# Attention block: one of two joins of the softmax sums on GpSimd, the steps behind it a burst later

## Chip, core and metric

The kernel runs on one core of a Trainium2 chip. The time is the device time of one execution in microseconds, as a median over runs. The engines are named as in the profile: PE (TensorE matmuls), PEld (its weight loads), DVE (VectorE), ACT (ScalarE), POOL (GpSimd) and SP (SyncE, which here only issues DMAs). Each engine works through its own queue in order; between engines, an instruction waits on semaphores of others.

## The reference

The input x has 4 images of 512 channels and 48 x 48 = 2304 positions. It is a group norm, a 1x1 convolution to q, k and v, attention with 8 heads of 64 channels over the 2304 positions, another 1x1 convolution and a residual:

```python
hn = _group_norm(x, gn_scale, gn_bias)                 # 32 groups
qkv = einsum('oc,bchw->bohw', qkv_w, hn) + qkv_b       # then to float16
w = einsum('bhct,bhcs->bhts', q * scale, k * scale)
w = softmax(w, axis=-1)
a = einsum('bhts,bhcs->bhct', w, v)                    # then to float32
return x + einsum('oc,bchw->bohw', proj_w, a) + proj_b
```

The softmax divides by the sum of exp(score) over the 2304 keys s, for each query position and head. How these sums are formed and applied is what the change is about. No maximum is subtracted in the fast path: the sums are tested against two limits, and if a test fails a general path (not run here) computes all again.

## The kernel before

Two heads are worked together (a pair), so there are 16 groups g: 4 images times 4 pairs. The queries of a group are cut into blocks j: four of 512 and a last, short one of 256. The keys of a block are gone through in bursts. A burst has three steps; each makes scores of 128 keys for both heads and 512 queries (for the short block 256 keys and 256 queries). A full block has 6 bursts, a short one 3, all together 432. The loop at the end of `fast_path` goes over the bursts n in this order and issues for each engine:

- `scores(n)`: 6 matmuls into three banks (`ps`), and three exponentials on ACT into a tile `p` of 128 x 3 x 1024 f16. There are three such tiles.
- `add(n-1)`: on DVE, the burst before is added to the block's accumulator `acc` (128 x 3072 f16, one buffer). The first burst of a block issues nothing; the second adds two `p` tiles at once (`acc<-p,p`). With the last burst the accumulator's three thirds are joined by two more additions (line 991).
- `values(n-2)`: 6 matmuls of v with `p` into the bank `av`, of which there is one; at the block's end DVE copies it to `avx` (line 968).
- `fill(n)`: other work of PE, from a list in a fixed order with costs and due times: chains for q and k of coming groups (line 711), for v (line 762) and for the output projection of the image before (line 839). All use one bank; DVE empties it after each chain (lines 721, 770, 866). A chain of q, k or v is in two pieces, so it is emptied every second burst; a projection chain is one piece. `fill` also issues small tasks for DVE ahead of that: statistics of the next image (line 610) and its normalization (line 662), in the stretches of the run where an image changes.

The joined sums still have to be added over the 128 partitions, inverted and brought to every partition. If E is the last burst of a block, this is done as follows. `add` of E with its joins comes in iteration E+1. In E+2 `turn` transposes the joined 128 x 1024 in blocks of 32 x 32 on DVE (line 1036), then come values of E and the copy to `avx`, then `fill`, and at the iteration's end `fold`: a sum along rows on DVE (line 1044, tile `part`) and four DMAs that bring its quarters to 32 partitions (`qs`). In E+3 `fill` is issued ahead of `values`, otherwise behind. In E+4 `invert_turned` has DVE's small steps (sum of the quarters, reciprocal, a small transposition, lines 1064, 1073, 1075), two DMAs to a row in DRAM, and POOL's tests of the limits (lines 1086, 1087). In E+5 `spread` broadcasts the row to 128 partitions by two DMAs (`ib<-row`), and in E+6 `divide` multiplies `avx` by it on POOL (line 1130) into the attention output `att`. 77 blocks go this way; the last three blocks of the run have their sums added on PE. The function `ready` tells from which burst after E a block's conversion to 32 bits (ACT, line 833) and its projection may start.

Since queues keep their order, a wait of the transposition on DVE holds back what is issued behind it: the emptying of the filling bank, the row sums and the first add of the next block. That first add in turn frees the `p` tile that ACT needs four bursts after E.

Of the kernel before, what the change touches and what calls it, by code (L numbers as in the profile page):

```python
# [17 lines left out]
ALU = mybir.AluOpType  # L18
# [11 lines left out]
NG = B * NPAIR  # L30
NT = T // P
SCALE = float(np.float16(1.0 / math.sqrt(math.sqrt(D))))
BURST = 3
BEHIND = 2
# [10 lines left out]
NQ = len(QBLOCKS)  # L45
# [422 lines left out]
def fast_path(  # L468
# [12 lines left out]
    nc = tc.nc  # L481

    RES = NC
    SQ = 32
# [424 lines left out]


    open_sums, joined = set(), set()
    av, acc, pts, avx, sums, rowd, ibs = {}, {}, {}, {}, {}, {}, {}

    stream = []
# [7 lines left out]
    def scores(u):  # L922
        g, j, k, _ = u
        o, n = QBLOCKS[j]
        per = QB // n
        qt, kt = qk[g]
        pt = ppool.tile([P, BURST, 2, QB], F16, tag="p", name=f"p_{g}_{j}_{k}")
        for r in range(BURST):
            ps = ps_s.tile([P, 2, QB], F32, tag="ps", name=f"ps_{g}_{j}_{k}_{r}")
            for a in range(per):  # L930
                i = (k * BURST + r) * per + a
                for h in range(2):
                    rows = slice(h * D, (h + 1) * D)
                    nc.tensor.matmul(  # L934
                        ps[:, h, a * n : (a + 1) * n],
                        kt[rows, bass.ts(i, P)],
                        qt[rows, o : o + n],
                        start=True,
                        stop=True,
                    )  # L940
            nc.scalar.activation(pt[:, r], ps, AF.Exp)  # L941
        pts[u] = pt

    def values(u):
        g, j, k, last = u
        b, pr = divmod(g, NPAIR)
        o, n = QBLOCKS[j]
        per = QB // n
        pt = pts.pop(u)
        if k == 0:  # L950
            if j == 0:
                atts[g] = apool.tile([P, T], F16, tag="att", name=f"att_{g}")
            av[0] = ps_av.tile([P, QB], F32, tag="av", name=f"av_{g}_{j}")
        for r in range(BURST):
            for a in range(per):
                i = (k * BURST + r) * per + a
                for h in range(2):
                    lo = h * D
                    nc.tensor.matmul(  # L959
                        av[0][lo : lo + D, :n],  # L960
                        vv[b, pr // 2][:, i, pr % 2 * P + lo : pr % 2 * P + lo + D],
                        pt[:, r, h, a * n : (a + 1) * n],
                        start=(i == 0),
                        stop=(i == NT - 1),
                    )
        if last and u is not stream[-1]:
            avx[g, j] = work.tile([P, QB], F32, tag="avx", name=f"avx_{g}_{j}")
            nc.vector.tensor_copy(avx[g, j][:, :n], av[0][:, :n])

    def add(u):  # L970

        g, j, k, last = u
        pt = pts[u]
        if k == 0:
            acc[g, j] = [pt]
            return
        if j >= NQ - 2 and g == NG - 1 and (last or j == NQ - 1):
            acc[g, j].append(pt)
            return
        before = acc[g, j][0]  # L980
        if k == 1:
            acc[g, j] = [
                work.tile(
                    [P, BURST, 2, QB], F16, tag="acc", bufs=1, name=f"acc_{g}_{j}"
                )
            ]
        t = acc[g, j][0]
        nc.vector.tensor_tensor(t, before, pt, ALU.add)  # L988
        if last:
            for r in range(1, BURST):  # L990
                nc.vector.tensor_tensor(t[:, 0], t[:, 0], t[:, r], ALU.add)  # L991
            joined.add((g, j))

    def add_up(g, j, bank=None, more=False):
# [38 lines left out]

    def turn(g, j):

        nc.vector.transpose(  # L1036
            t_turned(g, j).rearrange("p h n -> p (h n)"),
            acc[g, j][0][:, 0].rearrange("p h n -> p (h n)"),
        )

    def fold(g, j):

        part = small.tile([P, SQ], F32, tag="part", name=f"part_{g}_{j}")
        nc.vector.tensor_reduce(  # L1044
            part,
            t_turned(g, j).rearrange("p h (c k) -> p (h c) k", k=SQ),
            AX.X,
            ALU.add,
        )
        del acc[g, j]  # L1050
        quarters = small.tile([SQ, P // SQ, SQ], F32, tag="quarters", name=f"qs_{g}_{j}")
        for p in range(P // SQ):
            nc.sync.dma_start(quarters[:, p, :], part[bass.ts(p, SQ), :])  # L1053
        sums[g, j] = quarters

    def t_turned(g, j):
        return acc[g, j][0][:, 1]

    def invert_turned(g, j):
        n = QBLOCKS[j][1]  # L1060
# [57 lines left out]
    def spread(g, j):  # L1118
        n = QBLOCKS[j][1]
        row = rowd.pop((g, j))  # L1120
        ib = work.tile([P, QB], F32, tag="rows", name=f"ib_{g}_{j}")
        for h in range(2):
            nc.sync.dma_start(
                ib[h * D : (h + 1) * D, :n], row[h : h + 1, :n].to_broadcast((D, n))
            )
        ibs[g, j] = ib

    def divide(g, j):
        o, n = QBLOCKS[j]
        nc.gpsimd.tensor_tensor(  # L1130
            atts[g][:, o : o + n],
            avx.pop((g, j))[:, :n],
            ibs.pop((g, j))[:, :n],
            ALU.mult,
        )
# [37 lines left out]
    def do_tasks(room):  # L1173
        while tasks and tasks[0][0] <= now[0] and room > 0:
            _, us, run = tasks.popleft()
            run()
            room -= us
# [18 lines left out]
    def ready(b, j):  # L1196

        if b < B - 1:
            return BEHIND + 6
        return BEHIND + (4 if j == NQ - 3 else 5)  # L1200

    def put_convert(b, j):
        end = ends[((b + 1) * NPAIR - 1) * NQ + j]
        put(projs[b, j][0], end + ready(b, j))
# [15 lines left out]
    for b in range(B):  # L1220
        g = b * NPAIR
# [113 lines left out]
    def issue():  # L1335
        us, run = beside.pop(0)[:2]
        run()
        credit[0] -= us

    def fill(n):  # L1340

        idle = beside and beside[0][4] and not beside[0][4]()
        if ended(n - 1):
            room = 1.1 if idle else 0.0
        elif ended(n - BEHIND - 1):
            room = 1.1 if idle else 0.5
        else:  # L1350
            room = 2.4 if idle else 1.1
        do_tasks(room)
        rate, work = 0.0, 0.0
        for us, _, _, _, _, _, need in beside:
            work += us
            left = min(need * per_pair, len(stream) - 4) - n
            rate = max(rate, work / max(left, 1))
        credit[0] = min(credit[0] + rate, 4.0)
        closed = False
        while beside:  # L1360
            us, _, first, last, when, after, _ = beside[0]
            if after > n or (first and closed) or (when and not when()):
                break
            if us > 0.1 and credit[0] < us / 2:
                break
            issue()
            closed = closed or last
# [17 lines left out]
    def block_at(n):  # L1385

        return stream[n][:2] if ended(n) and n not in soon else None

    for n in range(end):
        now[0] = n  # L1390
        while loads and loads[0][0] <= n:
            loads.popleft()[1]()
        summed = block_at(n - BEHIND - 1)
        wanted(stream[n][0])
        scores(stream[n])
        if block_at(n - BEHIND):
            turn(*block_at(n - BEHIND))
        if n > 0:
            add(stream[n - 1])
        if summed:  # L1400

            fill(n)
        if n >= BEHIND:
            values(stream[n - BEHIND])
        if block_at(n - BEHIND - 2):
            invert_turned(*block_at(n - BEHIND - 2))
        if block_at(n - BEHIND - 3):
            spread(*block_at(n - BEHIND - 3))
        if block_at(n - BEHIND - 4):

            divide(*block_at(n - BEHIND - 4))
        if not summed:
            fill(n)
        if block_at(n - BEHIND):
            fold(*block_at(n - BEHIND))
        if n - BEHIND in soon:
            g, j = stream[n - BEHIND][:2]
            sx = rows(g, j, add_up(g, j))
            if n - BEHIND == soon[1]:
                divide_here(g, j, sx, avx[g, j], nc.gpsimd)  # L1420
        if n - BEHIND - 1 == soon[0]:
            check_sums(g, j)
            invert(g, j)
        if n - BEHIND - 2 == soon[0]:
            spread(g, j)
            divide(g, j)
    g, b, j = NG - 1, B - 1, NQ - 1
    n = QBLOCKS[j][1]
# [99 lines left out]
```

## Time and profile before

| | us |
|---|---|
| median of 3 runs | 1629.15 (1628.12 to 1629.5) |
| profiled execution | 1627.3 |
| its span | 1625.6 |
| PE busy | 1574.3 (97%) |
| DVE busy | 1319.5 (81%) |
| ACT busy | 1283.2 (79%) |
| POOL busy | 236.2 (15%) |
| both joins of a block, line 991, 156 instructions | 110.8, each 0.71 |
| transpositions, line 1036, 77 | 94.9, each 1.232 |
| row sums, line 1044, 77 | 92.8, each 1.205 |
| divisions on POOL, line 1130, 78 | 121.5, each 1.558 |

The busy time is that of the profiled execution, as a share of its span, which runs from the first to the last instruction. PE's clock was granted at 0.997 of full speed over the run. Busy times of different engines lie beside each other and don't add up to the span. In the groups of instructions a number after the bar is the idle time of that engine just ahead of them and what ended it; in the timeline each row has a start, a duration, engine, line, operation, tiles, and in brackets the idle time before with what ended it.

### The profile page before, as it was taken

How to read it: one execution, taken by the hardware profiler on the slowest of the kernel's cores; microseconds unless marked ns; L12 is line 12 of the kernel's file. 1: busy time of each engine (PE TensorE's matmuls, PEld its weight loads, DVE VectorE, ACT ScalarE, POOL GpSimd, SP SyncE). 2: the span in 40 equal slices, each digit the busy share in tenths (PEclk: the TensorE clock that was granted, in tenths of full speed). 3: DMA queues.
4: the chain of work that ended last, by engine and by line, in shares of the span. 5: the costliest groups of instructions: out<-in, count | busy, mean ns of one | idle time of the engine just before them, and what ended most of it. 6: DMA issues, size and time to landing. Idle time of an engine off the chain costs nothing.

```text
span 1625.6 us, 28473 instructions
## 1 busy us (share of the span) xinstructions
PE 1574.3 (97%) x11316; PEld 685.0 (42%) x11316; DVE 1319.5 (81%) x1533; ACT 1283.2 (79%) x1398; POOL 236.2 (15%) x434
## 2 busy tenths in 40 slices
PE   6999999999999999999999999999999999999996
PEld 2533434443333533545333353355533334434544
DVE  6278789978788889998778787999878887888885
ACT  3077787788888888887888888888878888888894
POOL 1000101221111111111111111101111121111112
PEclk9999999999999999999999999999999999999998
DMA  7002020000000023420000001343000000005413
GB/s 215 6 14 66 12 63 26 18 16 12 14 19 15 13 66 118 141 67 28 12 15 19 15 12 41 116 139 97 25 15 18 15 19 15 16 24 186 125 61 131
DMA packets 71011, 83.10 MB, mean 51 GB/s; under 512 B 26964, under 2 KB 37076, under 8 KB 70868
## 3 DMA queue, kind: packets, MB, share of 16 engines
q1 hardware_dynamic: 68836, 79.34, 16.0%
q8 instruction: 90, 1.47, 0.4%
q10 hardware_dynamic: 1904, 1.84, 0.4%
q14 instruction: 53, 0.43, 0.1%
q0 software_dynamic: 128, 0.01, 0.0%
HBM read 60.70 MB, written 19.17 MB: 49 GB/s over the span
## 4 chain that ended last, share of the span: by engine, by line
PE 72%; DVE 15%; ACT 4%; DMA 4%; issue 3%; SPq 2%; POOL 0%; DVEq 0%; ACTq 0%; POOLq 0%
PE pqk L711 26%; PE av L959 14%; PE pv L762 14%; PE ps L934 14%; DVE acc L988 4%; PE pr L839 3%; ACT p L941 3%; DVE part L1044 2%; PE ps L711 1%; SPq L1053 1%; DMA qs<-part 1%; DVE r L866 1%; DVE acc L991 1%; DMA r<-x_dram 1%; DVE k L721 1%
## 5 line engine op out<-in xcount | busy, mean ns | idle before, releaser
L941 ACT ACTIVATE p<-ps 128x1024 f16<-128x1024 f32 x1296 | 1231.9, 1027 | 306.7 <-PE ps L934 287.8
L711 PE MATMUL pqk<-x,wqkv 128*64 128x512 f32 (+1 forms) x2464 | 520.2, 552 | 8.8 <-DVE k L721 4.2
L988 DVE TENSOR_TENSOR acc<-acc,p 128x3072 f16<-128x3072 f16 x270 | 485.6, 1798 | 41.4 <-ACT p L941 37.9
L934 PE MATMUL ps<-q,k 64*128 64x512 f16 (+1 forms) x2880 | 359.5, 358 | 5.8 <-ACT p L941 5.1
L959 PE MATMUL av<-p,v 128*64 128x512 f16 (+1 forms) x2880 | 361.0, 364 | 0.4 <-DVE slx L1027 0.3
L762 PE MATMUL pv<-wqkv,x 128*64 128x256 f32 x2304 | 269.0, 380 | 4.6 <-DVE v L770 2.7
L711 PEld LDWEIGHTS pqk<-x,wqkv 128*64 128x64 f32 x2464 | 167.9, 137 | 238.9 <-issue 166.3
L934 PEld LDWEIGHTS <-k 64*128 64x128 f16 x2880 | 107.5, 94 | 297.4 <-issue 249.0
L959 PEld LDWEIGHTS <-v 128*64 128x64 f16 x2880 | 131.9, 109 | 210.6 <-issue 166.4
L762 PEld LDWEIGHTS pv<-wqkv,x 128*64 128x64 f32 x2304 | 159.8, 137 | 99.8 <-DVE v L770 8.5
L1086 POOL TENSOR_SCALAR tin<-tsum 32x32 f32<-32x32 f32 (+1 forms) x154 | 45.0, 292 | 953.1 <-DVE tsum L1064 947.9
L1130 POOL TENSOR_TENSOR att<-avx,ib 128x512 f16<-128x512 f32 (+1 forms) x78 | 121.5, 1558 | 353.4 <-DMA ib<-row 350.7
L988 DVE TENSOR_TENSOR acc<-p,p 128x3072 f16<-128x3072 f16 x79 | 139.8, 1769 | 8.0
L839 PE MATMUL pr<-a,whi 128*128 128x512 f32 (+1 forms) x312 | 121.9, 398 | 9.9 <-DVE r L866 5.0
L991 DVE TENSOR_TENSOR acc<-acc 128x1024 f16<-128x1024 f16 x156 | 110.8, 710 | 5.3
L839 PE MATMUL pr<-a,wlo 128*128 128x512 f32 (+1 forms) x312 | 114.4, 374 | 0.0
L770 DVE TENSOR_TENSOR v<-pv,bv 128x512 f16<-128x512 f32 x72 | 49.5, 688 | 70.0 <-PE pv L762 69.8
L721 DVE TENSOR_SCALAR q<-pqk,bqkv 128x512 f16<-128x512 f32 (+1 forms) x79 | 54.7, 693 | 60.8 <-PE pqk L711 59.8
L721 DVE TENSOR_SCALAR k<-pqk,bqkv 128x512 f16<-128x512 f32 (+1 forms) x75 | 51.6, 689 | 55.4 <-PE pqk L711 55.0
L1036 DVE STREAM_TRANSPOSE acc<-acc 128x1024 f16<-128x1024 f16 x77 | 94.9, 1232 | 0.6
L1044 DVE TENSOR_REDUCE part<-acc 128x32 f32<-128x1024 f16 x77 | 92.8, 1205 | 0.0
L839 PEld LDWEIGHTS pr<-a,whi 128*128 128x128 f32 x312 | 58.5, 188 | 48.3 <-DVE r L866 14.6
(70 smaller groups left out, 525.4 us busy)
## 6 DMA issues: line engine op xcount, KB each, us to landing
r<-x_dram SPq DMA_DIRECT2D x72, 256.0 KB
out_dram<-r SPq DMA_DIRECT2D x69, 256.0 KB
ib<-row SPq DMA_DIRECT2D x126, 128.0 KB
x<-x_dram SPq DMA_DIRECT2D x62, 256.0 KB
qs<-part SPq DMA_DIRECT2D x308, 4.0 KB
x<-x_dram SPq DMA_DIRECT2D x16, 128.0 KB
row<-tback SPq DMA_DIRECT2D x124, 2.0 KB
ib<-row SPq DMA_DIRECT2D x30, 64.0 KB
```

Source lines behind the costliest of these rows:

```text
L711: nc.tensor.matmul(pw[0][lo : lo + D, :n], wqkv[:, c, w0 + lo : w0 + lo + D], hn[b, c, j], start=(c == 0), stop=(c == NC - 1),)
L721: nc.vector.tensor_scalar(qk[g][part][:, o : o + n], pw[0][:, :n], bqkv[:, col : col + 1], SCALE, ALU.add, ALU.mult,)
L762: nc.tensor.matmul(pw[0][lo : lo + D, a, :], hn[b, c, i * P // QB][:, at + lo : at + lo + D], wqkv[:, c, 2 * C + half * C // 2 :][:, : C / ...
L839: nc.tensor.matmul(ps[:, :n], w[:, c, bass.ts(m, P)], at32[b, j, c], start=(i == 0), stop=(i == len(steps) - 1),)
L934: nc.tensor.matmul(ps[:, h, a * n : (a + 1) * n], kt[rows, bass.ts(i, P)], qt[rows, o : o + n], start=True, stop=True,)
L941: nc.scalar.activation(pt[:, r], ps, AF.Exp)
L959: nc.tensor.matmul(av[0][lo : lo + D, :n], vv[b, pr // 2][:, i, pr % 2 * P + lo : pr % 2 * P + lo + D], pt[:, r, h, a * n : (a + 1) * n], ...
L988: nc.vector.tensor_tensor(t, before, pt, ALU.add)
L991: nc.vector.tensor_tensor(t[:, 0], t[:, 0], t[:, r], ALU.add)
L1036: nc.vector.transpose(t_turned(g, j).rearrange("p h n -> p (h n)"), acc[g, j][0][:, 0].rearrange("p h n -> p (h n)"),)
L1044: nc.vector.tensor_reduce(part, t_turned(g, j).rearrange("p h (c k) -> p (h c) k", k=SQ), AX.X, ALU.add,)
L1130: nc.gpsimd.tensor_tensor(atts[g][:, o : o + n], avx.pop((g, j))[:, :n], ibs.pop((g, j))[:, :n], ALU.mult,)
```

## The change

The second of the two joins of a block goes from DVE to POOL, for all blocks but those from j = 2 on in the last group. In E+2 the transposition now comes after the copy to `avx`, and writes into the accumulator's second third as before. The row sums with their four DMAs move to iteration E+3, between `scores` and `add`. `invert_turned`, `spread` and `divide` each come an iteration later (E+5, E+6, E+7), and so does the earliest start that `ready` gives to conversion and projection. `fill` always comes last in an iteration; ahead of `values` in E+3 is gone.

```diff
-            for r in range(1, BURST):
+            turns = g < NG - 1 or j < NQ - 3
+            for r in range(1, BURST - 1 if turns else BURST):
                 nc.vector.tensor_tensor(t[:, 0], t[:, 0], t[:, r], ALU.add)
+            if turns:
+                nc.gpsimd.tensor_tensor(
+                    t[:, 0], t[:, 0], t[:, BURST - 1], ALU.add
+                )
...
     def turn(g, j):
-        nc.vector.transpose(
-            t_turned(g, j).rearrange("p h n -> p (h n)"),
-            acc[g, j][0][:, 0].rearrange("p h n -> p (h n)"),
-        )
+        t = acc.pop((g, j))[0]
+        turned[g, j] = t[:, 1].rearrange("p h n -> p (h n)")
+        nc.vector.transpose(turned[g, j], t[:, 0].rearrange("p h n -> p (h n)"))
...
         if b < B - 1:
-            return BEHIND + 6
-        return BEHIND + (4 if j == NQ - 3 else 5)
+            return BEHIND + 7
+        return BEHIND + (4 if j == NQ - 3 else 6)
...
-        summed = block_at(n - BEHIND - 1)
         wanted(stream[n][0])
         scores(stream[n])
+        if block_at(n - BEHIND - 1):
+            fold(*block_at(n - BEHIND - 1))
+        if n > 0:
+            add(stream[n - 1])
+        if n >= BEHIND:
+            values(stream[n - BEHIND])
         if block_at(n - BEHIND):
             turn(*block_at(n - BEHIND))
-        if n > 0:
-            add(stream[n - 1])
-        if summed:
-            fill(n)
-        if n >= BEHIND:
-            values(stream[n - BEHIND])
-        if block_at(n - BEHIND - 2):
-            invert_turned(*block_at(n - BEHIND - 2))
         if block_at(n - BEHIND - 3):
-            spread(*block_at(n - BEHIND - 3))
+            invert_turned(*block_at(n - BEHIND - 3))
         if block_at(n - BEHIND - 4):
-            divide(*block_at(n - BEHIND - 4))
-        if not summed:
-            fill(n)
-        if block_at(n - BEHIND):
-            fold(*block_at(n - BEHIND))
+            spread(*block_at(n - BEHIND - 4))
+        if block_at(n - BEHIND - 5):
+            divide(*block_at(n - BEHIND - 5))
+        fill(n)
```

More of the change, by code (lines that the diff above doesn't have):

```diff
@@ L911, in fast_path @@
     open_sums, joined = set(), set()
+    turned = {}
     av, acc, pts, avx, sums, rowd, ibs = {}, {}, {}, {}, {}, {}, {}
@@ L1045, in fold @@
             part,
-            t_turned(g, j).rearrange("p h (c k) -> p (h c) k", k=SQ),
+            turned.pop((g, j)).rearrange("p (c k) -> p c k", k=SQ),
             AX.X,
@@ L1049, in fold @@
         )
-        del acc[g, j]
         quarters = small.tile([SQ, P // SQ, SQ], F32, tag="quarters", name=f"qs_{g}_{j}")
@@ L1054, in fold @@
         sums[g, j] = quarters
-    def t_turned(g, j):
-        return acc[g, j][0][:, 1]
     def invert_turned(g, j):
```

## The prediction

> **What bounds the kernel now.** I read the shares of the engines first, then the costliest groups, then the timeline of PE and DVE around the end of a block.
>
> ```profile
> PE 1574.3 (97%) x11316; PEld 685.0 (42%) x11316; DVE 1319.5 (81%) x1533; ACT 1283.2 (79%) x1398; POOL 236.2 (15%) x434
> L1130 POOL TENSOR_TENSOR att<-avx,ib 128x512 f16<-128x512 f32 (+1 forms) x78 | 121.5, 1558 | 353.4 <-DMA ib<-row 350.7
> L991 DVE TENSOR_TENSOR acc<-acc 128x1024 f16<-128x1024 f16 x156 | 110.8, 710 | 5.3
> ```
>
> PE is the bound. DVE matters only where it hands something over late: a filling chain's bank (there is one) until DVE has emptied it, or p, which ACT refills. The table's busy share hides part of that, since the end of a matmul is modelled. So I took from PE's timeline the start of the first score matmul of each of the 432 bursts, and for bursts with the same filling the quickest fifth as the clean period: 3.24 us with half a q/k chain, 3.25 with half a v chain, 3.59 with a projection chain. What all bursts are longer than that is 39.4 us, the most that this change can reach. By the distance from a block's last burst E, behind full blocks and behind the short one (j = 4, three bursts): E+1 2.6 and 1.1 us; E+2 2.5 and 4.8; E+3 9.5 and 4.2; E+4 3.4 and 0; E+5 4.7 and 5.6; E+6 1.3 and 0.3 (the rest is rounding and the start). E+3 and E+5 hold most, and behind the short block E+2.
>
> The timeline at a short block's end (start, us, what):
>
> ```profile
> 947.39 1.42 DVE L991 TENSOR_TENSOR acc<-acc 128x1024 f16<-128x1024 f16 x2
> 948.73 0.36 DVE L1064 TENSOR_REDUCE tsum<-qs 32x32 f32<-32x128 f32 x1
> 949.63 0.64 DVE L770 TENSOR_TENSOR v<-pv,bv 128x512 f16<-128x512 f32 x1
> 950.20 1.22 DVE L1036 STREAM_TRANSPOSE acc<-acc 128x1024 f16<-128x1024 f16 x1
> 950.32 1.95 PE L762 MATMUL pv<-wqkv,x 128*64 128x256 f32 x16 [0.37 <-DVE v L770]
> ```
>
> Two joins, then the small steps of the block before (with 0.58 us for their DMA) stand ahead of the emptying at 949.63, and PE waits for it. A full block:
>
> ```profile
> 532.10 1.42 DVE L991 TENSOR_TENSOR acc<-acc 128x1024 f16<-128x1024 f16 x2
> 533.55 1.25 DVE L1036 STREAM_TRANSPOSE acc<-acc 128x1024 f16<-128x1024 f16 x1
> 533.59 0.84 PE L959 MATMUL av<-p,v 128*64 128x512 f16 x6
> 534.72 0.65 DVE L968 COPY avx<-av 128x512 f32<-128x512 f32 x1
> 536.21 0.69 DVE L770 TENSOR_TENSOR v<-pv,bv 128x512 f16<-128x512 f32 x1 [0.84 <-PE pv L762]
> 536.82 1.21 DVE L1044 TENSOR_REDUCE part<-acc 128x32 f32<-128x1024 f16 x1
> 538.13 1.76 DVE L988 TENSOR_TENSOR acc<-p,p 128x3072 f16<-128x3072 f16 x1
> ```
>
> Here DVE has room until 536, then runs emptying, row sums and first add without a gap.
>
> **The change part by part.** PE's instructions are the same, burst for burst; only at E+3 do filling and values change places, 77 times. Start, tail and projection order stay.
>
> *The join on POOL.* DVE loses 77 x 0.71 = 54.7 us. POOL takes 1.27 us for 512 elements and 0.73 for 256 when nothing disturbs it (the many att rows at these values), so 2.11 ns an element and 2.35 us for 1024. No f16 addition on POOL is in the trace. Bounds: 0.71, what DVE takes, and 3.9 (2.35 and the longest stretch seen, 1.5 us, of an att at 1497.73). I take 2.35: the same engine, operation class and rows. After the first join DVE has only emptyings, which read PSUM, so nothing should stretch it.
>
> What waits: the transposition, and behind it in DVE's queue the emptying of E+2, row sums, first add. Counted from the joins' start, POOL ends at 0.71 + 0.05 + 2.35 = 3.1 us. DVE gets to the transposition once values of E are done (median 2.5) and copied (0.65): median 3.05, quartiles 2.9 and 3.6, over 77 blocks. So it waits in 43 blocks, 14.6 us in all, 0.2 each. The transposition ends at about 4.4, where the old order had transposition and copy done by 3.3 to 5.0. The row sums and the first add come 0.7 us later on average.
>
> *Emptying at E+2, short blocks.* It no longer stands behind the second join (0.71) and the small steps (0.93 and their DMA wait): 1.6 us earlier, against losses of 0.4 to 0.7 in eight places. −4.5 of 4.8.
>
> *E+3.* Filling now comes after values, so PE asks for the bank 0.77 us later. Filling of E+2 ends at (values' end + 1.8); it is asked for again 1.5 later, was 0.75. In the full block above: filling ends at 3.9, transposition at 4.4, emptying at 5.1, asked for at 5.4: no loss. Of 77 blocks 14 with a real loss remain, all but one with statistics, norms or small steps now between transposition and emptying. Worst is 1040.80: transposition to 4.4, steps 0.93, statistics 1.25, emptying 0.72 make 7.3 against 5.1 asked, so 2.3 lost where 1.4 was. Block by block this comes to 12.3 us; the same reckoning of the old order gives 11.5 where 13.6 was lost, but 0.4 too much at each of eight projection bursts. Corrected to 9.0: −4.6.
>
> *First add later.* It frees p for ACT. In the full block: row sums to 6.4, add to 8.2 from the joins; ACT could start at 9.5, in lighter spots at 7.9. Summed, ACT starts 23.6 us late. PE feels what passes 0.47 us (a score bank's third part is asked 3.74 us after the burst's start and released at 3.27): 9 us, of which 4 fall in bursts already lost at E+3. +5.
>
> *Small steps, spread and division a burst later.* The small steps (0.97 on DVE) leave E+4 and come in at E+5. At E+4 DVE is 0.7 late for the reason above and gains 0.97; at E+5 it pays it. Bounds for the 10.3 us lost at E+5: −6 if lateness is made up, +4 if it moves on. I take 0. qs and part now have a burst more to land: DVE's waits for qs (5.3 us) go, inside these terms. On SP a short block's four qs now go ahead of the ib of the block before, which so waits for the row sums, up to a burst; its reader, the division, is a burst later as well, and the loads of x and residuals behind it in the queue are issued bursts ahead of their use. On POOL the division stands behind the next block's join and ends about 4.4 us after that block's joins begin; avx and ib have two buffers and the copies to a32 come a burst later too: 0.
>
> *Division beside DVE.*
>
> ```profile
> 602.07 1.26 POOL L1130 TENSOR_TENSOR att<-avx,ib 128x512 f16<-128x512 f32 x1 [5.89 <-DMA ib<-row]
> 602.45 2.50 DVE L988 TENSOR_TENSOR acc<-acc,p 128x3072 f16<-128x3072 f16 x1 [0.78 <-ACT p L941]
> ```
>
> An add that begins during a division takes 2.50 instead of 1.75; a division that begins during an add takes up to 2.8. The 270 adds average 1798 ns against a median of 1749: 13 us. The division now falls on copy and transposition, not adds. DVE gains those 13 us, PE by it perhaps −0.5 (0 to −2).
>
> [...]
>
> Sum: −4.5 − 4.6 + 5 + 0 − 0.5 = −4.6 us. The profiled execution took 1627.3 us (span 1625.6), 1.85 below the median of 1629.15; so 1622.7 for it and **1624.5** for the median. About 0.2% (3.3 us) is what a measurement can tell from no change.
>
> **The rivals.** (1) The join is longer than its cover, slower. At 3.0 us, DVE waits 51 us instead of 14.6 at 67 of 77 transpositions, and the E+3 reckoning gives 29.6 instead of 12.3: +17, about 1642. The gain is used up at 2.6 us, slower by 0.2% from about 2.75. For it: no f16 row, and the cover fits to 0.1 us. Against: two att sizes on one line. (2) The stretches with statistics and norms (260–380, 620–740, 1040–1160) give the gain back: there DVE is busy 93% (111.66 of 120 us at 620–740), E+5's losses come back at E+6, and 17 blocks have the first add 1.1 us later. A quarter of those 18.7 us more on PE: about 1629, no change. (3) All of the 18.7 lands on PE: +14 over my sum, about 1638, slower. Against: PE's own losses there move its demands back too.
>
> **How the numbers follow.** Forecast case 0.43 (1618 to 1626), rival 2 0.25, rival 1 0.20, rival 3 0.12. Hence faster 0.43, same 0.25, slower 0.32. The low end, 1617, is the sum with E+5's better bound (−6) and the division's (−2): −12; the high end, 1641, leaves out the far half of rival 1.
>
> **What would show it.** POOL's acc rows near 2.35 us and DVE's transposition starting within 0.3 us of their end; L988 near 1750 ns; no wait of PE on the emptying 2.9 us behind a short block's join; ACT's waits for the first add above 18.7 us. Wrong if the join is over 2.6, or if PE's waits grow in the three dense stretches.

## The result, and the profile after

The changed kernel takes 1627.41 us (1626.79 to 1629.56, 12 runs) against 1627.86 (1626.4 to 1629.6, 12 runs) of the kernel before: ratio 0.9999, 95% interval 0.999 to 1.0008. No change can be measured. The profiled execution took 1627.17 us, its span is 1625.4.

The shares of the engines and the costliest groups of the kernel after (busy time, mean ns of one, idle time ahead and what ended it):

```profile
PE 1572.3 (97%) x11316; PEld 684.5 (42%) x11316; DVE 1250.3 (77%) x1456; ACT 1282.3 (79%) x1398; POOL 410.4 (25%) x511
...
L989 DVE TENSOR_TENSOR acc<-acc,p 128x3072 f16<-128x3072 f16 x270 | 472.5, 1750 | 34.7 <-ACT p L942 32.1
...
L995 POOL TENSOR_TENSOR acc<-acc 128x1024 f16<-128x1024 f16 x77 | 163.6, 2125 | 489.0 <-DVE acc L993 484.7
...
L1131 POOL TENSOR_TENSOR att<-avx,ib 128x512 f16<-128x512 f32 (+1 forms) x78 | 100.8, 1292 | 122.9 <-DMA ib<-row 122.9
...
L1044 DVE STREAM_TRANSPOSE acc<-acc 128x1024 f16<-128x1024 f16 x77 | 95.2, 1236 | 4.3 <-POOL acc L995 4.1
```

DVE has 69 us less to do and the time stays: DVE's load as a whole was not the bound. The join takes 2.13 us on POOL. The transposition waits for it 4.1 us in all. The adds are no longer stretched by divisions (mean 1750 ns; before, 1798). Of the 78 divisions 13 still take 0.2 us or more above their shortest time, before 38 (means 1292 and 1558 ns); each of the 13 begins during an add.

The waits of the kernel after (total us, times, longest):

```profile
ACT p L942 <- DVE acc L989: 36.8, 32, 3.0
DVE tback L1076 <- POOL tinv L1073: 11.3, 15, 1.3
DVE acc L1044 <- POOL acc L995: 4.1, 9, 1.0
```

ACT waits for adds twice as long as before (18.7 us). The second line is new.

The same short block as in the prediction, timeline of the kernel after (start, us, what):

```profile
946.76 0.69 DVE L993 TENSOR_TENSOR acc<-acc 128x1024 f16<-128x1024 f16 x1
947.60 2.13 POOL L995 TENSOR_TENSOR acc<-acc 128x1024 f16<-128x1024 f16 x1 [8.08 <-DVE acc L993]
947.70 0.69 DVE L770 TENSOR_TENSOR v<-pv,bv 128x512 f16<-128x512 f32 x1 [0.25 <-PE pv L762]
...
949.02 1.89 PE L762 MATMUL pv<-wqkv,x 128*64 128x256 f32 x16
949.29 0.42 DVE L969 COPY avx<-av 128x256 f32<-128x256 f32 x1 [0.90 <-PE av L960]
949.76 1.25 DVE L1044 STREAM_TRANSPOSE acc<-acc 128x1024 f16<-128x1024 f16 x1
950.92 0.32 DVE L1065 TENSOR_REDUCE tsum<-qs 32x32 f32<-32x128 f32 x1
```

The emptying (947.70) now waits for PE and not PE for it, and the filling at 949.02 starts without a wait. POOL is done at 949.73, when the copy to `avx` ends: the join is just covered. But the small steps of the block before (950.92) now stand behind the transposition, ahead of the next emptying. What that does where statistics are due as well shows the short block at 1040, also of the kernel after:

```profile
1040.99 2.13 POOL L995 TENSOR_TENSOR acc<-acc 128x1024 f16<-128x1024 f16 x1 [8.98 <-DVE acc L993]
...
1042.08 0.43 DVE L969 COPY avx<-av 128x256 f32<-128x256 f32 x1 [1.24 <-PE av L960]
1043.15 1.25 DVE L1044 STREAM_TRANSPOSE acc<-acc 128x1024 f16<-128x1024 f16 x1 [0.64 <-POOL acc L995]
...
1044.32 0.33 DVE L1065 TENSOR_REDUCE tsum<-qs 32x32 f32<-32x128 f32 x1
...
1045.19 1.23 DVE L610 BATCH_NORM_STATS2 st<-x 128x6 f32<-128x512 f32 x2
...
1046.35 0.72 DVE L721 TENSOR_SCALAR q<-pqk,bqkv 128x512 f16<-128x512 f32 x1
1047.00 1.20 DVE L1049 TENSOR_REDUCE part<-acc 128x32 f32<-128x1024 f16 x1
1047.13 1.95 PE L711 MATMUL pqk<-x,wqkv 128*64 128x256 f32 x16 [1.92 <-DVE q L721]
1048.30 1.76 DVE L989 TENSOR_TENSOR acc<-p,p 128x3072 f16<-128x3072 f16 x1
...
1050.16 2.85 ACT L942 ACTIVATE p<-ps 128x1024 f16<-128x1024 f32 x3 [1.62 <-DVE acc L989]
```

Transposition, small steps, two statistics and only then the emptying: PE loses 1.92 us, and the first add behind them makes ACT lose 1.62.

The same timeline a few bursts earlier, in E+2 to E+4 of the full block ahead, shows where the loss at E+1 behind short blocks comes from:

```profile
1033.54 0.68 DVE L610 BATCH_NORM_STATS2 st<-x 128x6 f32<-128x512 f32 x1
1034.13 1.20 DVE L1049 TENSOR_REDUCE part<-acc 128x32 f32<-128x1024 f16 x1
1035.43 1.76 DVE L989 TENSOR_TENSOR acc<-p,p 128x3072 f16<-128x3072 f16 x1
1037.11 0.69 DVE L610 BATCH_NORM_STATS2 st<-x 128x6 f32<-128x512 f32 x1
1037.29 2.85 ACT L942 ACTIVATE p<-ps 128x1024 f16<-128x1024 f32 x3 [1.26 <-DVE acc L989]
1037.71 0.74 DVE L721 TENSOR_SCALAR k<-pqk,bqkv 128x512 f16<-128x512 f32 x1
1038.50 1.94 PE L711 MATMUL pqk<-x,wqkv 128*64 128x512 f32 x8 [0.92 <-DVE k L721]
```

A short block has three bursts, so its E+1 is E+4 of the full block ahead of it, where the first add is late. Of the rise from 1.1 to 2.9 us 1.6 lie in two bursts, this one and one at 281 us.

With the prediction's measure (burst periods over the same clean periods), what PE loses, in us, behind full / short blocks. It is read from one execution of each kernel; over the 14 profiles, span less loss agrees to some 3 us, so differences of 1 or 2 us in the whole loss tell little:

| | E+1 | E+2 | E+3 | E+4 | E+5 | E+6 | all |
|---|---|---|---|---|---|---|---|
| before | 2.6 / 1.1 | 2.5 / 4.8 | 9.5 / 4.2 | 3.4 / 0.0 | 4.7 / 5.6 | 1.3 / 0.3 | 39.4 |
| after | 2.9 / 2.9 | 1.7 / 0.8 | 5.6 / 8.0 | 8.2 / 1.5 | 1.4 / 2.6 | 1.8 / 2.3 | 39.1 |

("All" takes in the rounding and the start, about −0.5.) So the change takes some 15 us of loss away at some places, adds as much at others, and the sum stays. Outside the three stretches with statistics and norms the loss falls from 20.1 to 17.2, within them it rises from 19.3 to 21.8; according to which bursts at their edges are counted, the rise is between 0.7 and 3.1.

### The profile page after: what moved, and what is told of

The parts are those of the page before. It is cut to its first block, busy times and chain, and to the rows that moved or that the text cites. A ratio compares the mean times of both kernels' runs of the same rounds, so it can differ in the third digit from the quotient of the medians.

```text
span 1625.4 us, 28489 instructions
## 1 busy us (share of the span) xinstructions
PE 1572.3 (97%) x11316; PEld 684.5 (42%) x11316; DVE 1250.3 (77%) x1456; ACT 1282.3 (79%) x1398; POOL 410.4 (25%) x511
## 4 chain that ended last, share of the span: by engine, by line
PE 73%; DVE 12%; ACT 6%; issue 3%; DMA 2%; POOL 2%; SPq 1%; DVEq 0%; ACTq 0%; POOLq 0%
PE pqk L711 25%; PE av L960 15%; PE ps L935 15%; PE pv L762 13%; ACT p L942 5%; PE pr L839 4%; DVE acc L989 4%; POOL acc L995 1%; DVE part L1049 1%; PE ps L711 1%; DVE acc L1044 1%; DMA x<-x_dram 1%; ACT a L833 1%; DMA ib<-row 1%; DVE st L610 1%
## 5 line engine op out<-in xcount | busy, mean ns | idle before, releaser
L989 DVE TENSOR_TENSOR acc<-acc,p 128x3072 f16<-128x3072 f16 x270 | 472.5, 1750 | 34.7 <-ACT p L942 32.1
L995 POOL TENSOR_TENSOR acc<-acc 128x1024 f16<-128x1024 f16 x77 | 163.6, 2125 | 489.0 <-DVE acc L993 484.7
L960 PEld LDWEIGHTS <-v 128*64 128x64 f16 x2880 | 125.7, 108 | 203.9 <-issue 164.5
L1087 POOL TENSOR_SCALAR tin<-tsum 32x32 f32<-32x32 f32 (+1 forms) x154 | 72.3, 470 | 527.6 <-DVE tsum L1065 521.1
L989 DVE TENSOR_TENSOR acc<-p,p 128x3072 f16<-128x3072 f16 x79 | 138.9, 1758 | 8.4 <-ACT p L942 0.5
L1131 POOL TENSOR_TENSOR att<-avx,ib 128x512 f16<-128x512 f32 (+1 forms) x78 | 100.8, 1292 | 122.9 <-DMA ib<-row 122.9
L969 DVE COPY avx<-av 128x512 f32<-128x512 f32 (+1 forms) x79 | 50.6, 641 | 86.2 <-PE av L960 83.0
```

The lines of the kernel that those rows point to most:

```text
L960: nc.tensor.matmul(av[0][lo : lo + D, :n], vv[b, pr // 2][:, i, pr % 2 * P + lo : pr % 2 * P + lo + D], pt[:, r, h, a * n : (a + 1) * n], ...
L995: nc.gpsimd.tensor_tensor(t[:, 0], t[:, 0], t[:, BURST - 1], ALU.add)
L1131: nc.gpsimd.tensor_tensor(atts[g][:, o : o + n], avx.pop((g, j))[:, :n], ibs.pop((g, j))[:, :n], ALU.mult,)
```

## The experiments

Each ratio is against runs of the kernel before taken together with it; "after" means the changed kernel, from which every edit starts. PE's order of work is that of after in all of them. The expectations name theories by letters.

**Both joins on DVE.**

```diff
-            for r in range(1, BURST - 1 if turns else BURST):
+            for r in range(1, BURST):
...
-            if turns:
-                nc.gpsimd.tensor_tensor(t[:, 0], t[:, 0], t[:, BURST - 1], ALU.add)
```

> The changed kernel with the second join back on DVE and nothing else undone. Theory A (the join's place does not matter, because the transposition now waits for the values and their copy: median 3.05 us after the joins' start, when two joins on DVE end at 1.42): the transposition starts within 0.3 us of where it does in the changed kernel, PE's loss over clean burst periods stays within 2 us of the changed kernel's 39.1, time within 0.1% of it. Theory B (the 53 us taken from DVE are what pays for the later first add): DVE busy rises by about 55 us and the time by 3 to 6 us.

Measured: 1628.36 us, ratio 1.0021 (1.0012 to 1.003), PE's loss 42.4 us. E+3 fell to 2.3 / 3.9, but E+2 behind full blocks rose from 1.7 to 11.9. Theory A missed; the time is what theory B forecast, but the cause is another. It is in the groups and in the timeline of this kernel, here around a full block's joins:

```profile
L992 DVE TENSOR_TENSOR acc<-acc 128x1024 f16<-128x1024 f16 x156 | 149.2, 957 | 5.3
```

```profile
529.29 1.75 DVE L989 TENSOR_TENSOR acc<-acc,p 128x3072 f16<-128x3072 f16 x1
530.14 2.02 POOL L1126 TENSOR_TENSOR att<-avx,ib 128x512 f16<-128x512 f32 x1 [2.83 <-DMA ib<-row]
531.07 2.37 DVE L992 TENSOR_TENSOR acc<-acc 128x1024 f16<-128x1024 f16 x2
```

The division, a burst later than before, begins during the last add (which runs until 531.04) and so takes 2.02 us instead of 1.28; the two joins, which begin during the division, take 2.37 instead of 1.42. In after it can't, because in POOL's queue it stands behind the join, which waits for DVE. So the join on POOL does something that the prediction had not put down to it: it keeps the division away from DVE's join.

**Small steps, spread and division back at E+4, E+5, E+6.**

```diff
-        if block_at(n - BEHIND - 3):
-            invert_turned(*block_at(n - BEHIND - 3))
+        if block_at(n - BEHIND - 2):
+            invert_turned(*block_at(n - BEHIND - 2))
...
```

(`spread` and `divide` likewise one burst earlier.)

> The changed kernel with small steps, spread and division at their old distances (E+4, E+5, E+6). Theory A (the delay takes PE's loss out of E+5 and behind short blocks out of E+2, and puts it behind short blocks into E+3): losses at E+5 return to about 10 us (from 4.0), E+3 behind short blocks falls from 8.0 to about 4.5, since the steps then fill the wait for the values; sum +1 to +3 us. Theory B (the delay is neutral, losses follow the first add only): no position moves by more than 1.5 us.

Measured: 1627.63 us, ratio 1.0012 (1.0003 to 1.0021; after: 0.9999), loss 41.0 us: E+3 5.5 / 2.8, E+4 8.8 / 0.9, E+5 4.9 / 9.2, E+6 0.6 / 0.2. As theory A had it, putting the steps off is worth 10 us at E+5 and costs 5 at E+3 behind short blocks and 3 at E+6.

**The new order alone:** both edits above together, so that only filling, values, transposition, row sums and first add stand as in after.

> The new order of filling, values, row sums and first add alone: both joins on DVE, small steps, spread and division at their bursts of before. The division then meets the adds as before (add rows mean near 1800 ns) and not the joins (156 of them near 710). Theory C goes on to say that putting off the division pays only with something on POOL that holds it back: without either, E+2 loses about 2 behind full and 1 behind short blocks, E+3 about 3 and 3, E+4 7 to 9, E+5 5 and 9 as with the early steps and the join on POOL; in all about 36 us, ratio 0.9985 to 1.000, better than the kernel with both joins on DVE (1.0021) and worse than that with the small POOL addition (0.9976). Rival (putting off the steps is worth nothing): ratio 0.997 to 0.998, with E+5 below 6 us in all.

Measured: 1633.03 us, ratio 1.0037 (1.0025 to 1.005), loss 44.4 us. Both expectations missed. The adds and joins are as expected (means 1791 and 723 ns) and E+3 is at its best (3.3 / 1.3), but E+2 behind short blocks costs 7.4 us, not 1. Timeline of this kernel at the short block shown above:

```profile
948.52 1.42 DVE L992 TENSOR_TENSOR acc<-acc 128x1024 f16<-128x1024 f16 x2
949.85 0.35 DVE L1060 TENSOR_REDUCE tsum<-qs 32x32 f32<-32x128 f32 x1
...
950.75 0.64 DVE L770 TENSOR_TENSOR v<-pv,bv 128x512 f16<-128x512 f32 x1
...
951.44 1.95 PE L762 MATMUL pv<-wqkv,x 128*64 128x256 f32 x16 [0.50 <-DVE v L770]
```

Second join and small steps stand ahead of the emptying, as before the change. Taking either away is enough (E+2 behind short blocks 1.3 with the join on POOL, 0.9 with the steps put off): the two parts buy the same 6 us, not twice.

**A small POOL addition in place of the join**, to hold the division back: both joins on DVE, and behind them on POOL

```diff
+                nc.gpsimd.tensor_tensor(
+                    t[:, 2, 0, :8], t[:, 0, 0, :8], t[:, 0, 1, :8], ALU.add
+                )
```

> The kernel with both joins on DVE, and a POOL addition of 8 elements that reads what the second DVE join wrote, so that POOL's division can no longer begin while the joins run. Theory C (what the join on POOL buys is not its own 0.71 us of DVE but that it stands in POOL's queue ahead of the division and keeps it off the joins): the 156 joins come back from a mean of 957 ns to about 700, the loss at E+2 behind full blocks falls from 11.9 to about 3 us while E+3 stays near 2.3 and 3.9, the loss in all is about 33 us and the time about 9 us below that of the kernel with both joins on DVE, ratio near 0.996 to the kernel before. Rival (taking the second join off DVE is what counts): E+2 stays above 8 us and the time stays at or above that of the changed kernel, ratio 0.9999 or more. The small addition writes a part of the accumulator that nobody reads.

Measured: 1622.5 us, ratio 0.9976 (0.9967 to 0.9985), loss 33.8 us: E+2 1.8 / 1.0, E+3 3.8 / 3.9. Groups, and the same full block:

```profile
L993 DVE TENSOR_TENSOR acc<-acc 128x1024 f16<-128x1024 f16 x156 | 108.9, 698 | 5.3
L995 POOL TENSOR_TENSOR acc<-acc 128x8 f16<-128x8 f16 x77 | 15.2, 198 | 562.3 <-DVE acc L993 562.3
```

```profile
530.09 1.42 DVE L993 TENSOR_TENSOR acc<-acc 128x1024 f16<-128x1024 f16 x2
...
531.59 0.20 POOL L995 TENSOR_TENSOR acc<-acc 128x8 f16<-128x8 f16 x1 [5.26 <-DVE acc L993]
531.75 1.27 POOL L1131 TENSOR_TENSOR att<-avx,ib 128x512 f16<-128x512 f32 x1
```

Theory C holds: 0.20 us of POOL behind the joins brings the joins back to 698 ns and the loss at E+2 back to that of after. Against this kernel the real join on POOL costs 5.3 us of loss: 5.9 more at E+3, of which 4.1 lie behind the nine blocks whose transposition waited for it 4.1 us, and 0.6 less elsewhere. The ratios fit together:

| | steps at the old bursts | steps a burst later |
|---|---|---|
| both joins on DVE | 1.0037 | 1.0021 |
| second join on POOL | 1.0012 | 0.9999 (after) |
| both on DVE, division held back | not run | 0.9976 |

The new order alone costs 0.37%. The steps a burst later gain 0.13 to 0.16%. The join on POOL gains 0.22 to 0.25%; with the steps late, that is 0.45% gained by holding the division back and 0.23% lost by its own 2.1 us. Every ratio has an interval of about ±0.1%, so the first of these differences is hardly more than its own uncertainty; the 0.45% is well outside it.

**A longer join:** one more addition of 384 elements on POOL ahead of the join, into a part that the transposition overwrites. This adds work.

> The changed kernel with an extra POOL addition of 384 elements (written to the part of the accumulator that the transposition overwrites) ahead of the join, so that POOL ends the join 0.95 us later, at about 3.9 us from the first join's start instead of 2.9. It shows what the wait of the transposition costs when the join is longer than its cover (the forecast's first rival). By the forecast's block by block reckoning DVE's waits for POOL rise from 4 to about 55 us, loss at E+3 by 15 to 20 us and the time as much. Rival: DVE's idle time later in the block takes it up, under +6 us.

Measured: 1665.3 us, ratio 1.0233 (1.0219 to 1.0247), loss 77.0 us, 41.2 of them at E+3. Groups of this kernel, then its waits:

```profile
L995 POOL TENSOR_TENSOR acc<-acc 128x384 f16<-128x384 f16 x77 | 70.1, 911 | 484.0 <-DVE acc L993 484.0
```

```profile
ACT p L942 <- DVE acc L989: 65.9, 44, 3.1
DVE acc L1047 <- POOL acc L998: 45.5, 58, 2.0
```

0.91 us more on POOL cost 38 us. DVE's wait for the join grows by 41 us and PE's loss by 38: beyond 2.1 us there is no slack left. Rival 1's mechanism is real; at 2.13 us the join escapes most of it, all but the 4.1 us named above.

**Tasks in the join's cover:** statistics and norms are refused at E+2 instead of at E+1.

```diff
-        if ended(n - 1):
+        if ended(n - BEHIND):
```

> The changed kernel with statistics and norms kept out of E+2 (between transposition and emptying) and let into E+1 (behind the first join, while POOL joins). PE's order of work stays. Theory A (the stretches with these tasks give the gain back because they stand ahead of emptying, row sums and first add): loss in those stretches falls from 21.8 us to about 17, E+4 behind full blocks from 8.2 to about 4.5, and up to 2 us return at E+2; time -2 to -4 us. Theory B (DVE is simply full there, the place of the tasks is no matter): loss there within 1.5 us of 21.8.

Measured: 1629.45 us, ratio 1.0028 (1.0016 to 1.0039). E+4 fell from 8.2 / 1.5 to 3.6 / 1.2, and E+2 behind full blocks rose from 1.7 to 10.5. So tasks ahead of a late first add are 4.6 of the 8.2 us at E+4, and of the loss at E+1 behind short blocks too, which falls from 2.9 to 1.3. The places were right, but what is taken from one burst is paid at another: the loss in all is 38.6 us, 0.5 less than in after. That profile is of an execution of 1626.37 us, 3 us below the median of the seven; where the longer ones lose more, no trace shows.

**Small steps ahead of the values**, so of the transposition too:

```diff
+        if block_at(n - BEHIND - 3):
+            invert_turned(*block_at(n - BEHIND - 3))
         if n >= BEHIND:
             values(stream[n - BEHIND])
```

> The changed kernel with the small steps issued ahead of values and copy in their iteration; this alters DVE's order only behind short blocks, where they then run in the wait for the values instead of between transposition and emptying. Theory A: E+3 behind short blocks falls from 8.0 us to about 5, E+4 and E+6 there by 1 together; time -2 to -4 us. Theory B (the first add is late for the transposition alone): under 1 us.

Measured: 1622.04 us, ratio 0.9981 (0.9972 to 0.9991), loss 33.9 us; E+3 behind short blocks 2.9 instead of 8.0, E+5 behind them 1.3 instead of 2.6, E+6 3.9 instead of 2.3. This shows what the steps' new place costs: they fit into DVE's time while POOL joins, and stood behind it.

**The ones written by DVE.** `invert_turned` sets 16 columns to one by a POOL instruction in 15 blocks; it stands behind the division and so behind the division's wait for `ib` (11.3 us in the waits of after).

```diff
-            nc.gpsimd.memset(inv[:, 2 * cols :], 1.0)
+            nc.vector.memset(inv[:, 2 * cols :], 1.0)
```

> The changed kernel with the small setting of ones for short blocks (line 1073) on DVE instead of POOL, where it stands behind the division and so behind the DMA of ib. Theory A (a queue that the forecast overlooked: DVE's small transposition waits 11.3 us for it at 15 places, which loses PE's time at E+6 behind short blocks): that wait goes, loss at E+6 behind short blocks falls from 2.3 us to below 1, time -1 to -3 us. Theory B (the wait falls into DVE's own idle time): no change beyond 0.5 us.

Measured: 1629.3 us, ratio 1.0018 (1.0009 to 1.0027), loss 40.3 us. The wait goes and the time doesn't: E+6 behind short blocks stays at 2.3, as theory B had it. The time even rises, which neither theory had, and part of that lies outside the span. In the four kernels with the ones on DVE an execution takes 2.2 to 3.4 us more than its span (medians 2.8 to 3.0), in all others 1.7 to 2.0. The cause of these 1.2 us or so is not known. By the medians of the spans, this kernel's ratio is 1.0010.

**First add ahead of the row sums** in E+3 (the transposition then writes a tile of its own, so that the add may overwrite the accumulator).

```diff
-        if block_at(n - BEHIND - 1):
-            fold(*block_at(n - BEHIND - 1))
         if n > 0:
             add(stream[n - 1])
+        if block_at(n - BEHIND - 1):
+            fold(*block_at(n - BEHIND - 1))
```

> The changed kernel with the transposition writing into another tile (a buffer of the division's), so that the next block's first add need not wait for the row sums and is issued ahead of them; row sums and their DMAs come 1.8 us later. Theory A (the losses that the change brings at E+4 are ACT waiting for p until the first add): ACT's waits for it fall from 36.8 us to under 15, loss at E+4 behind full blocks from 8.2 to about 4; time -3 to -5 us. Theory B (the emptying that comes late is what costs there): under 1 us.

Measured: 1631.12 us, ratio 1.0027 (1.0017 to 1.0037). ACT's waits of 36.8 us are gone but for 3.1, and still E+4 falls only to 6.6 / 1.0: most of the loss there is not ACT's wait for the first add. And another wait has grown; the waits of this kernel:

```profile
DVE tback L1076 <- POOL tinv L1073: 30.6, 15, 3.7
```

E+6 behind short blocks rises to 10 us: the ones on POOL now matter. All three edits together, and then the first two of them:

> The changed kernel with three alterations together: small steps ahead of values (which alone took 5 us off PE's loss), ones on DVE, and the first add ahead of the row sums. If the three act at different places of a block, as theory A has it, PE's loss falls to about 27 us and the time is 10 to 12 us (0.7%) below the changed kernel's. Theory B (a delay taken out at one place comes back at the next): no more than 5 us below.

Small steps first, ones on DVE, first add first: 1619.4 us, ratio 0.9954 (0.994 to 0.9967), loss 31.3 us: some 7 us below, between the two forecasts. E+6 behind short blocks is 4.3.

> The changed kernel with the small steps ahead of the values and the ones on DVE, the row sums still ahead of the first add. It splits the gain of the fastest kernel (0.9954) against that of the small steps alone (0.9981). Theory (the order of add and row sums carries it): ratio 0.997 to 0.998, ACT's waits for the first add stay above 30 us. Rival (POOL's memset behind the division carries it, now that nothing else of the small steps stands there): ratio 0.995 to 0.996.

Without the first add first: 1621.91 us, ratio 0.9974 (0.9964 to 0.9985), ACT waits 32.4 us. So the order of add and row sums gives 0.1 to 0.2%, once the ones are off POOL's queue (0.9974 and 0.9954; 0.9962 and 0.9948 by spans). The ones by themselves give nothing that these intervals can show (0.9981 and 0.9974); by spans it is 0.9979 and 0.9962, so what they gain inside the span may be lost again outside it.

> The fastest kernel so far (small steps ahead of the values, ones on DVE, first add ahead of the row sums; ratio 0.9954), with the join on POOL put back on DVE and the same POOL addition of 8 elements behind it. Theory C: the transposition no longer waits for a join of 2.1 us on POOL, so the loss behind full blocks at E+3 (5.6 us) falls by about 3 us and nothing is lost at E+2: ratio 0.993 to 0.995. Rival (the second join on DVE costs as much as it saves, since DVE's 0.71 us stand ahead of the emptying at E+2 behind short blocks, where 4.8 us were lost before the change): ratio 0.996 to 0.998.

All three edits, both joins on DVE and the small POOL addition: 1616.55 us, ratio 0.9948 (0.9934 to 0.9961), loss 27.6 us, E+3 4.0 / 3.5. It is the fastest kernel of the study and faster than the one with the small POOL addition alone (0.9976). Its interval overlaps that of the kernel with the join on POOL (0.9954), so whether theory C's last step adds to the other three is not settled by the times; the losses of one execution each say 3.7 us.

## Why the prediction was right and wrong

The time fell into the range, 2.9 us above the point. That it came so near is in part luck: the forecast was a change of −4.6 us, measured is −0.45, and the median of three runs from which it started lay 1.3 us above that of twelve. The likeliest case, faster, did not come; rival 2 did, no change, with part of the gain given back in the dense stretches, and so did one of the signs that the prediction named for being wrong, PE losing more there. By the prediction's own terms:

| term | forecast | measured |
|---|---|---|
| E+2 behind short blocks | −4.5 | −4.0 |
| E+3 | −4.6 | 0 (−3.9 full, +3.8 short) |
| first add later (E+4) | +5 | +6.2 |
| small steps a burst later (E+5) | 0, from −6 to +4 | −6.3 |
| division beside DVE | −0.5 | in the other rows |
| E+1, E+6, E+2 behind full blocks | no term | +2.1, +2.5, −0.8 |
| sum | −4.6 | −0.3 |

- **The join.** Taken at 2.35 us from the rate of the divisions, it measured 2.125: 1.9 ns an element (from the additions of 1024 and 384) and not the 2.11 of the divisions. DVE's emptyings left it alone, as foreseen: in after 52 of the 77 joins ran beside one, and all 77 took 2.12 to 2.14 us. It ended 2.9 us after the joins' start (532.78 to 535.68 in the full block), not 3.1, so the transposition waited in 9 blocks for 4.1 us, not in 43 for 14.6. What each 0.2 us is worth there, the longer join shows: the cover was put right, the price of missing it too low. At 51 us of DVE's waits the forecast for rival 1 had PE lose 17 us more; measured, waits of 45.5 us went with 38.
- **E+3 is the step that failed.** "Corrected to 9.0: −4.6": measured 13.6, as before the change. The block-by-block reckoning had given 12.3. For the old order it had given 11.5 where 13.6 was lost, so it was 2.1 too low in all; the correction took off the 3.3 by which it was too high at projection bursts and left out the 5.4 by which it was too low elsewhere. Moved by the whole difference, 12.3 becomes 14.4, and the sum of all terms +0.8: no change. What costs there, two runs show: behind short blocks the loss rose to 8.0; 2.9 is left when the steps are issued earlier (the small steps ahead of the values), and 3.9 when the transposition need not wait for the join (the small POOL addition). Either is enough for most of it, so the two prices lie on each other. Part of this the prediction had seen ("small steps now between transposition and emptying"); it then spread the price over 14 blocks and corrected it away.
- **E+4 was right in size, but its path is shown only for a small part.** The prediction has ACT wait for p and PE for its score banks. With the first add ahead of the row sums ACT hardly waits, and 7.6 of the 9.7 us stay. In after, PE waits in these bursts behind full blocks 3.9 us for the emptying of the filling bank and 2.1 for score banks, and with the first add first it still waits 2.6 and 2.1. That the size fits is in part luck.
- **E+5 at 0** was the middle of two true effects, of which the prediction had to choose one: the lateness does move on (with the steps early E+5 rises from 10.3 to 14.1, +3.8), and the steps taken away from it give back 10.1. The mechanism was given, the sum lies at the better bound.
- **E+6 and E+1 had no term.** The steps' cost goes on to E+6 behind short blocks (+2.0; 0.2 with the steps early). E+1 behind short blocks lost 1.1 before and loses 2.4 to 3.0 in nearly every kernel with the new order, but 1.3 where tasks are refused at E+2 instead. As the timeline at 1037 shows, it is the lateness at E+4 of the full block ahead once more; with it the first add's term measures +8.0 and not +6.2.
- **"DVE gains those 13 us, PE by it perhaps −0.5"** came true for the adds, by the lateness of the division alone (1757 ns in the kernel with both joins on DVE too). But the prediction let the division stand behind the next block's join and costed that at 0. It is worth 0.45%: without anything of the joins on POOL the late division falls on DVE's joins. The prediction had weighed a meeting of POOL and DVE for the new join and for the adds alone. The rows show what it costs DVE's joins (0.71 us in the mean before, 0.957 with both joins on DVE), while 55 copies of 512 elements to `avx` that ran beside a division in after took 0.69 us each, and 45 transpositions 1.23 to 1.25.
- **Steps shown right:** the emptying at E+2, L989 at 1750 ns, ACT's waits above 18.7 us (36.8), and of rival 2 the outcome and the place: E+5's losses came back partly at E+6, and the dense stretches lost 2.5 us where the others gained 2.9. But the stretches are not all of it: of the 5.2 us that the small steps ahead of the values bring back, about 4 lie outside them.

## What to carry to other kernels

When instructions are moved along an in-order queue whose engine is nearly full in some stretches, add up the loss of every burst that receives one, up to the point where the queue runs empty, before counting the gain of the burst that is relieved; and if two parts of a change relieve the same burst, count it once. Ask of each instruction on another engine what it holds back in that engine's queue: here a 0.2 us addition with both joins on DVE gained twice what the 2.1 us join on POOL gained. A cover that fits to a tenth of a microsecond is worth measuring by lengthening the work under it, because beyond its end nearly every microsecond that is waited can be lost (with the longer join 38 of 41).

## What was not expected of the hardware

- An f16 addition of 1024 elements on POOL takes 2.12 to 2.14 us in after, one of 384 takes 0.91 and one of 8 takes 0.20: some 0.2 us and 1.9 ns an element. The same addition takes 0.69 us on DVE, a third of it.
- Two joins on DVE that begin during a division on POOL: 1.42 us become 2.37, although their operands and the division's are different tiles. The division itself, begun 0.9 us before the end of an add on DVE, takes 2.02 us instead of 1.28.
- A POOL instruction of 0.1 us that waits for nothing itself (the ones) delayed DVE by 11.3 us in 15 blocks, and by 30.6 in another order. In 14 of the 15 blocks the instruction ahead of it was a division that had waited for a DMA.
- With that instruction of 0.1 us on DVE instead (0.07 us there), four kernels take about 1.2 us more outside their spans than all others; why is not known.
